# Two graph layers on one core: products read on the way from one growing bank, in a fixed order woven into the next stage

## The chip, the cores and the metric

The kernel runs on one core of a Trainium2 chip. TensorE (PE in the profile) multiplies, with its weight loads listed apart as PEld; VectorE (DVE), ScalarE (ACT) and GpSimd (POOL) do the element work; SyncE (SP) issues most of the transfers. The metric is the device time of one execution in microseconds (us). The kernel before took 1896.66 us, the median of three runs (1894.19 to 1897.85).

## The reference

For 64 graphs of 256 nodes with 512 features, an attention layer masked by the adjacency matrix and then a normalised graph convolution, each with a layer norm and a residual sum. Everything is float32.

```python
h = jnp.maximum(_layernorm(x, axis=-1), 0.0)
query = h @ Wq_w.T + Wq_b;  keyt = h @ Wk_w.T + Wk_b;  value = h @ Wv_w.T + Wv_b
weight = adj * jnp.exp(query @ keyt^T)
weight = weight / jnp.sum(weight, axis=2, keepdims=True)
x = x + weight @ value

h = jnp.maximum(_layernorm(x, axis=-1), 0.0)
A_hat = adj + I;  d = A_hat.sum(-1) ** -0.5
x = x + (A_hat * d[:, None] * d[None, :]) @ (h @ W + b)
```

(Shortened: batch indices left out.)

## The kernel before

**Pairs.** The 64 graphs go in 32 pairs (`NP`). The 512 rows of a pair lie in four tiles of 128 partitions. Query and key weights are merged once into one matrix, so that only one projection ("key", `m_set`) stands between the features and the scores; the value projection (`v_set`) and the graph weight (`w1_set`) are the other two.

**Seven products.** Each product of 512x512 matrices is done as seven products of half-size blocks instead of eight (the Winograd form of Strassen's method). Sums of blocks are made beforehand on both sides: S1 to S4 on the left, T1 to T4 on the right. The seven products are then added up in a fixed pattern. One product of a projection is 8 matmul records (4 matmuls in float32, two records each) of 128x256; one gather of the convolution, and one product of the scores, is 8 records of 128x128. The results lie in PSUM banks of 512 columns.

**How the sums were formed.** `seven_products` (L370) uses three banks. The first product P1 is copied out by ScalarE (`a1`). Later products land in other banks, and VectorE adds `a1` to two of them on the way (`s2`, `s3`, the temporaries U2 and U3), which are then added to the finished banks. For the keys (`key_side`, L385) the finished sums go into `gT` with a bias per row, for the values (`values`, L435) into `v`. In the convolution (`convolve`, L640) `gather` makes A_hat times h, transposed, in one bank that is read on the way (`chain`), and `product` multiplies by the graph weight; the results are scaled by the degree factor `d` and added to `x` by VectorE (L674) and GpSimd (L684).

**What runs beside it, per pair.**
- `measure`: layer-norm statistics of the next pair (`bn_stats`, `bn_aggr`), row sums of its adjacency (`degrees`), and the inverse roots on GpSimd (`inverse_root`, a chain of small operations); a small round trip through DRAM on SP for the degree row
- `normed`: relu of the layer norm on ScalarE, `h_a` for the first layer and `h_b` for the second
- `blocks_transposed` (`hq`) on VectorE and 16 `move_quadrants` copies on ScalarE: the transposed features `hT`
- `feature_sums`, `key_sums` and `neighbour_sums`: the block sums, on GpSimd from the second pair on (for the keys `eng = nc.vector if p == 0 else nc.gpsimd`)
- `key_terms` (`hc`, L281), `weighted_degrees` (`ad`, L597) and `add_graph_bias` (L614) on VectorE, each with two tensors in SBUF as its inputs
- `attend`: scores, exponentials on ScalarE, masks on VectorE, the output products (`pm_o`), and the residual sum; after it the diagonal of the adjacency is raised by one on GpSimd (L854)

**Order.** The program text is unrolled and a scheduler puts each engine's instructions in an order when the kernel is built; each engine then works its queue in that order. `tc.issue_after(ins)` keeps what is written inside it behind `ins` on that instruction's own engine, without a semaphore. Work for the neighbouring pairs is passed into the stages as callbacks (`then`, `then_u2`, ...), which write it down behind one of the stage's own reads. Nothing fixed the order of the matmuls of different stages against each other. In the loop, pair p attends, then pair p+1 is projected, then pair p is convolved.

**Buffers.** `x` has three, `a` (adjacency) and `hT` two, most temporaries one (`A0`, `A1`, `U2`, `U3`). The next adjacency load on SP waits for the last reader of its buffer, which is `weighted_degrees`; the next `x` load waits for the store of the pair that leaves.

Of the kernel before, what the change touches and what calls it, by code (L numbers as in the profile page):

```python
# [16 lines left out]
def kernel(  # L17
# [216 lines left out]
    last_root = [None]  # L234

    def inverse_root(src, plus, name):
# [4 lines left out]
        last_root[0] = nc.gpsimd.tensor_tensor(r, s, minus_half, ALU.pow).ins  # L241
        return r

    def scale_offset(p, name, scale=None):
# [3 lines left out]
        for t in range(TB):  # L248
            st = sm.tile([P, 6], F32, tag="st", name=f"st_{name}_{t}")
            nc.vector.bn_stats(st, xt[:, t, :])  # L250
            nc.vector.bn_aggr(mv[:, t, :], st)
# [24 lines left out]
    def key_terms(p, h):  # L276

        acc = sm.tile([P, TB], F32, tag="ka", name=f"ka_{p}")
        scratch = p1.tile([P, D], F32, tag="A0", name=f"hc_{p}")
# [48 lines left out]
    def key_sums(p, gT):  # L328
# [5 lines left out]
        eng = nc.vector if p == 0 else nc.gpsimd  # L334
# [5 lines left out]
        return (a11, a12, a22, s1, s2, a21, s4)  # L340

    def products_of(name, w, weight_moves):
# [6 lines left out]
        def product(bank, which, part, start):  # L349
# [3 lines left out]
            for r in range(2):  # L353
                for dt in range(2):
# [3 lines left out]
                    nc.tensor.matmul(  # L358
# [11 lines left out]
    def seven_products(name, w, parts, weight_moves, first, u2, c11, u3, c22, c21, c12):  # L370

        b11, b21, b22, t1, t2, t3, t4 = parts
        product = products_of(name, w, weight_moves)
        first(product(0, A11, b11, True))
        u2(product(1, S2, t2, True))
        c11(product(0, A12, b21, False))
        u3(product(1, S3, t3, False))
        c22(product(2, S1, t1, True))
        c21(product(1, A22, t4, False))
        return c12(product(2, S4, b22, False))  # L380

# [3 lines left out]
    def key_side(p, parts, then, then_u2, then_u3):  # L385
        gT = p1.tile([P, DC, NT], F32, tag="gT", name=f"gT_{p}")
        a1, s2, s3 = (temp(tag, f"g{p}") for tag in ("A1", "U2", "U3"))
# [4 lines left out]
        def block(i, g):  # L392
            return gT[:, 2 * i : 2 * i + 2, ts(g, N)]

        def first(pm):
            with tc.issue_after(nc.scalar.copy(a1, pm).ins):  # L396
                then()

        def u2(pm):
            with tc.issue_after(nc.vector.tensor_tensor(s2, pm, a1, add).ins):  # L400
                then_u2()

        def u3(pm):
            with tc.issue_after(nc.vector.tensor_tensor(s3, pm, a1, add).ins):  # L404
                then_u3()

        def c11(pm):
            for r in range(2):
                nc.scalar.activation(
                    block(0, 0)[:, r, :], pm[:, r, :], AF.Identity, bias=bias(0, r)  # L410
                )

        def into(i, g, pm, more):
# [375 lines left out]
    def nothing():  # L789
        pass  # L790
# [159 lines left out]
```

## Time and profile before

| | |
|---|---|
| median of three runs | 1896.66 us (1894.19 to 1897.85) |
| the profiled execution | 1896.71 us, span 1894.9 us |
| granted TensorE clock | 0.997 |
| VectorE busy | 1358.7 us, 72% |
| ScalarE busy | 797.9 us, 42% |
| GpSimd busy | 1070.3 us, 56% |
| PE, w products (L358) | 413.2 us, 1792 records of 386 ns |
| ACT, moves into hT (L311) | 305.5 us, 496 of 616 ns |
| DVE, hc (L281) | 115.9 us, 128 of 905 ns |
| DVE, graph bias (L614) | 94.5 us, 128 |
| POOL, idle before its first w sum (L708) | 410.1 us in 31 |

The span is the time from the first to the last instruction. The profile repeats itself: a pair takes 57.7 us from one key product to the next, from pair 2 to the last but one. The records of neighbouring matmuls overlap by some 0.16 us, since the end of each is modelled; for what a stage costs, the distance between starts is read. A figure in brackets behind a line is the idle time of that engine just before, and what ended it.

### The profile page before, as it was taken

To read this page: it belongs to the slowest core of one execution; us is meant where nothing else is said; L and a number is where in the kernel's file an instruction comes from. 1 tells how busy PE (TensorE), PEld (TensorE's weight loads), DVE (VectorE), ACT (ScalarE), POOL (GpSimd) and SP (SyncE) were. 2 spreads that over 40 slices of the span, in tenths; PEclk is the share of its full clock that TensorE was granted. 3 is DMA by queue.
4 is the path that set the end of the run, shared out by engine and by line. 5 is a ranking of instruction groups with operands and counts; after the bars stand their busy time and mean duration, and the time that the engine had idled before them with its cause. 6 is when DMAs were issued, how large, how long until landed. Compare 5 with 4: busy or idle time off the path is not lost.

```text
span 1894.9 us, 27986 instructions
## 1 busy us (share of the span) xinstructions
PE 1852.5 (98%) x10114; PEld 1642.0 (87%) x10114; DVE 1358.7 (72%) x3130; ACT 797.9 (42%) x1476; POOL 1070.3 (56%) x1191
## 2 busy tenths in 40 slices
PE   8999999999999999999999999999999999999997
PEld 7888888888888888888888888888888888888886
DVE  7877677677777676776777776777776767767764
ACT  3444443344444344434444443454344444434412
POOL 3545556646557555566465565555564555655544
PEclk9999999999999999999999999999999999999999
DMA  8243133332243432343422434413434323344011
GB/s 222 40 106 84 47 76 83 91 95 65 48 95 78 95 88 52 68 92 81 95 74 40 93 78 95 94 48 65 95 78 95 80 46 82 80 93 95 29 23 45
DMA packets 224266, 148.42 MB, mean 78 GB/s; under 512 B 150272, under 2 KB 170752, under 8 KB 224128
## 3 DMA queue, kind: packets, MB, share of 16 engines
q1 hardware_dynamic: 206112, 112.03, 22.3%
q0 software_dynamic: 16960, 33.56, 11.5%
q8 instruction: 80, 1.31, 0.3%
q10 hardware_dynamic: 1056, 1.05, 0.2%
q14 instruction: 58, 0.48, 0.1%
HBM read 112.99 MB, written 33.62 MB: 77 GB/s over the span
## 4 chain that ended last, share of the span: by engine, by line
PE 73%; DVE 25%; issue 1%; POOL 1%; DMA 1%; ACT 0%; DVEq 0%; ACTq 0%; POOLq 0%
PE pm_w L358 21%; PE pm_g L358 20%; PE pm_s L511 10%; PE pm_o L566 10%; DVE hc L281 6%; PE pm_v L358 6%; PE pm_l L654 5%; DVE hq L292 4%; DVE ad L597 3%; DVE x L614 2%; DVE wT L532 1%; DVE U_l L696 1%; DVE yS L694 1%; DVE U_v L446 1%; DVE v L472 1%; DVE v L471 1%
## 5 line engine op out<-in xcount | busy, mean ns | idle before, releaser
L358 PE MATMUL pm_w<-w_set,yS 128*128 128x256 f32 x1792 | 413.2, 386 | 3.8 <-DVE U_w L674 3.8
L358 PEld LDWEIGHTS pm_w<-w_set,yS 128*128 128x128 f32 x1792 | 332.4, 191 | 57.3 <-issue 10.4
L311 ACT COPY hT<-hq 32x512 f32<-32x512 f32 x496 | 305.5, 616 | 17.7 <-DVE hq L292 11.9
L708 POOL TENSOR_TENSOR yS<-yS 128x512 f32<-128x512 f32 x32 | 41.1, 1284 | 410.1 <-DVE yS L707 410.1
L358 PE MATMUL pm_v<-v_set,hT 128*128 128x256 f32 x1024 | 245.2, 382 | 10.3 <-DVE v L458 7.5
L358 PE MATMUL pm_g<-hT,m_set 128*128 128x256 f32 x1024 | 238.5, 381 | 4.2 <-DVE gT L415 4.2
L566 PE MATMUL pm_o<-v,wT 128*128 128x257 f32 (+1 forms) x1024 | 235.3, 382 | 3.5
L358 PEld LDWEIGHTS pm_v<-v_set,hT 128*128 128x128 f32 x1024 | 192.3, 190 | 47.5 <-DVE v L458 19.2
L566 PEld LDWEIGHTS pm_o<-v,wT 128*128 128x128 f32 x1024 | 189.1, 190 | 40.3 <-DVE wT L532 16.0
L358 PEld LDWEIGHTS pm_g<-hT,m_set 128*128 128x128 f32 x1024 | 195.7, 191 | 31.9 <-DVE gT L415 5.0
L358 PE MATMUL pm_g<-hS,m_set 128*128 128x256 f32 x768 | 181.2, 379 | 1.0 <-DVE U_g L404 1.0
L358 PE MATMUL pm_v<-v_set,hS 128*128 128x256 f32 x768 | 176.8, 379 | 0.0
L358 PEld LDWEIGHTS pm_g<-hS,m_set 128*128 128x128 f32 x768 | 145.7, 190 | 21.3 <-DVE U_g L404 1.4
L358 PEld LDWEIGHTS pm_v<-v_set,hS 128*128 128x128 f32 x768 | 146.0, 190 | 19.7
L674 DVE SCALAR_TENSOR_TENSOR x<-pm_w,irr_d,x 128x256 f32<-128x256 f32 x256 | 110.7, 475 | 52.1 <-PE pm_w L358 48.7
L684 POOL TENSOR_TENSOR x<-x,U_w 128x512 f32<-128x512 f32 x64 | 81.0, 1267 | 93.5 <-DVE U_w L674 93.5
L674 DVE SCALAR_TENSOR_TENSOR U_w<-pm_w,irr_d,A_w 128x256 f32<-128x256 f32 x128 | 56.0, 480 | 98.8 <-PE pm_w L358 98.8
L396 ACT COPY A_g<-pm_g 128x512 f32<-128x512 f32 x32 | 18.7, 585 | 245.2 <-PE pm_g L358 244.5
L281 DVE SCALAR_TENSOR_TENSOR hc<-h_a,c_all 128x512 f32<-128x512 f32 x128 | 115.9, 905 | 2.0
L267 ACT ACTIVATE h_b<-x,nb_b,rs_b 128x512 f32<-128x512 f32 x128 | 93.8, 803 | 47.9 <-POOL nb_b L260 47.9
L576 DVE SCALAR_TENSOR_TENSOR x<-pm_o,rsum,x 128x256 f32<-128x256 f32 x256 | 110.5, 474 | 1.1
L654 PE MATMUL pm_l<-aT,h_b 128*128 128x128 f32 x768 | 98.6, 278 | 10.6 <-DVE U_l L696 10.6
(157 smaller groups left out, 3342.8 us busy)
## 6 DMA issues: line engine op xcount, KB each, us to landing
x<-in_x_dram SPq DMA_DIRECT2D x64, 512.0 KB, 4.8
x<-in_L_gnn_Wv_b_dram POOLq DMA_DIRECT2D x32, 1024.0 KB, 10.5
out_dram<-x SPq DMA_DIRECT2D x62, 512.0 KB, 3.6
a<-in_adj_dram SPq DMA_DIRECT2D x64, 256.0 KB, 3.0
aq<-in_adj_dram SPq DMA_DIRECT2D x124, 128.0 KB, 5.4
drow<-dflat SPq DMA_DIRECT2D x32, 256.0 KB, 4.7
wq_rows<-in_L_gnn_Wq_w_dram ACTq DMA_DIRECT2D x2, 512.0 KB, 7.7
wk_rows<-in_L_gnn_Wk_w_dram SPq DMA_DIRECT2D x2, 512.0 KB, 7.0
```

Source lines behind the costliest of these rows:

```text
L267: nc.scalar.activation(h[:, t, :], x_tiles[p][:, t, :], AF.Relu, bias=nb[:, t : t + 1], scale=rd[:, t : t + 1],)
L281: nc.vector.scalar_tensor_tensor(scratch, h[:, t, :], 1.0, c_all, mult, mult, accum_out=acc[:, t : t + 1])
L292: nc.vector.transpose(hq[:, t, :], h[:, t, :])
L311: last = nc.scalar.copy(dst[j * Q : (j + 1) * Q, i], src[i * Q : (i + 1) * Q, j])
L358: nc.tensor.matmul(banks[bank][:, r, :], left[:, ts(r, P)], right, start=start and r == 0 and dt == 0, stop=r == 1 and dt == 1, skip_group ...
L511: nc.tensor.matmul(banks[bank][:, g, :], left[:, dt, ts(g, P)], right[:, dt, ts(g, P)], start=start and g == 0 and dt == 0, stop=g == 1 an ...
L566: nc.tensor.matmul(pm[:, 0:width], wT[:, kb, qb, g, :], v[:, kb * G + g, lo : lo + width], start=kb == 0, stop=kb == NB - 1,)
L576: nc.vector.scalar_tensor_tensor(xh, pm[:, 0:HD], rsum, xh, mult, add)
L597: nc.vector.scalar_tensor_tensor(scratch.rearrange("p (nb q) -> p nb q", q=P), a[:, t, :].rearrange("p (nb q) -> p nb q", q=P), 1.0, row_o ...
L654: nc.tensor.matmul(banks[bank][:, fi, g, :], left[:, g, ts(fi, P)], right[:, g, :], start=start and fi == 0 and g == 0, stop=fi == 1 and g ...
L674: last = nc.vector.scalar_tensor_tensor(dst[:, r, :], pm[:, r, :], dr_, plus[:, r, :], mult, add)
L684: last = nc.gpsimd.tensor_tensor(block(i, nb), block(i, nb), more, add).ins
```

## The change

The key and value projections no longer go through `seven_products`. A function `projections` writes both out in one fixed order. Per projection one bank grows: P1, then P1+P6, then P1+P6+P7 and so on are accumulated in it, and ScalarE copies the state out in between (`a`, `u2`, `u3`); the copies are added to the other banks by VectorE. The convolution's w products do the same with `wchain`. Every matmul of projections and convolution is kept behind the one before it in the text by `in_order`. The value projection's first product is placed among the keys, and the convolution of the pair before begins (two gathers) inside the value projection, by `filler`. Callbacks are replaced by a table of named places. The key sums are on VectorE for all pairs, `neighbour_sums` is split into `adjacency_sums` and `node_sums`, both on GpSimd, and graph bias, degree sums, statistics, the second norm, moves and weight sums have new places.

```diff
-        scratch = p1.tile([P, D], F32, tag="A0", name=f"hc_{p}")
+        scratch = p1.tile([P, D], F32, tag="U3", name=f"hc_{p}")
...
-        eng = nc.vector if p == 0 else nc.gpsimd
+        eng = nc.vector
+    last_product = [None]
+    def in_order(*args, **kwargs):
+        with tc.issue_after(last_product[0]) if last_product[0] else ExitStack():
+            last_product[0] = nc.tensor.matmul(*args, **kwargs).ins
...
-                    nc.tensor.matmul(
+                    in_order(
...
-    def seven_products(name, w, parts, weight_moves, first, u2, c11, u3, c22, c21, c12):
-        b11, b21, b22, t1, t2, t3, t4 = parts
-        product = products_of(name, w, weight_moves)
-        first(product(0, A11, b11, True))
-        u2(product(1, S2, t2, True))
-        c11(product(0, A12, b21, False))
-        u3(product(1, S3, t3, False))
-        c22(product(2, S1, t1, True))
-        c21(product(1, A22, t4, False))
-        return c12(product(2, S4, b22, False))
...
+        def key_sum(i, g, pm, more):
             for r in range(2):
                 last = nc.vector.scalar_tensor_tensor(
-                    block(i, g)[:, r, :], pm[:, r, :], bias(i, r), more[:, r, :], add, add
+                    key_block(i, g)[:, r, :], pm[:, r, :], bias(i, r), more[:, r, :], add, add
                 )
             return last
...
+        a, u2, u3 = (temp(tag, f"g{p}") for tag in ("A1", "U2", "U3"))
+        chain = keys_of(0, A11, b11, True)
+        behind(nc.scalar.copy(a, chain), "key P1")
+        rest = keys_of(2, S1, t1, True)
+        keys_of(0, S2, t2, False)
+        behind(nc.scalar.copy(u2, chain), "key P6")
+        side = keys_of(1, A12, b21, True)
+        behind(key_sum(0, 0, side, a), "key C11")
+        keys_of(0, S3, t3, False)
+        behind(nc.scalar.copy(u3, chain), "key P7")
+        behind(key_sum(1, 1, rest, u3), "key C22")
+        va = temp("A0", f"v{p}")
+        vchain = values_of(0, A11, b11, True)
+        nc.scalar.copy(va, vchain)
+        keys_of(0, A22, t4, False)
+        for r in range(2):
+            last = nc.scalar.activation(
+                key_block(1, 0)[:, r, :], chain[:, r, :], AF.Identity, bias=bias(1, r)
+            )
+        behind(last, "key C21")
+        keys_of(2, S4, b22, False)
+        last = key_sum(0, 1, rest, u2)
+        keys[p] = gT
+        behind(last, "key C12")
+        vu2, vu3 = (temp(tag, f"v{p}") for tag in ("A1", "U2"))
+        vrest = values_of(2, S1, t1, True)
+        values_of(0, S2, t2, False)
+        behind(nc.scalar.copy(vu2, vchain), "value P6")
+        vside = values_of(1, A12, b21, True)
+        behind(nc.vector.tensor_tensor(value_block(0, 0), vside, va, add), "value C11")
+        values_of(0, S3, t3, False)
+        behind(nc.scalar.copy(vu3, vchain), "value P7")
+        behind(nc.vector.tensor_tensor(value_block(1, 1), vrest, vu3, add), "value C22")
+        filler()
+        values_of(0, A22, t4, False)
+        nc.vector.tensor_copy(value_block(1, 0), vchain)
+        values_of(2, S4, b22, False)
+        nc.vector.tensor_tensor(value_block(0, 1), vrest, vu2, add)
...
-    def neighbour_sums(p, h, aT):
...
+    def adjacency_sums(p, aT):
...
+        nc.gpsimd.tensor_tensor(t1, b12, b11, sub)
+        nc.gpsimd.tensor_tensor(t2, b22, t1, sub)
+        nc.gpsimd.tensor_tensor(b12, b22, b12, sub)
+        nc.gpsimd.tensor_tensor(t4, b21, t2, sub)
+        return (b11, b21, b22, t1, t2, b12, t4)
+    def node_sums(p, h):
+        a11, a21 = h[:, 0:G, 0:HD], h[:, 0:G, HD:D]
+        a12, a22 = h[:, G:TB, 0:HD], h[:, G:TB, HD:D]
+        hbS = p1.tile([P, 3, G, HD], F32, tag="hbS", name=f"hbS_{p}")
+        s1, s2, s4 = (hbS[:, i] for i in range(3))
+        nc.gpsimd.tensor_tensor(s1, a21, a22, add)
+        nc.gpsimd.tensor_tensor(s2, s1, a11, sub)
+        nc.gpsimd.tensor_tensor(a21, a11, a21, sub)
+        last = nc.gpsimd.tensor_tensor(s4, a12, s2, sub)
+        if p == 0:
+            with tc.issue_after(last.ins):
+                weight_sums(w1_set, w1_21, nc.gpsimd)
+        return (a11, a12, a22, s1, s2, a21, s4)
+    def convolution(p, left_parts, right_parts, d, then):
...
+        def scaled(tag, pm, nb):
+            dst = temp(tag, f"w{p}")
+            for r in range(G):
+                last = nc.scalar.mul(dst[:, r, :], pm[:, r, :], factor(nb, r))
+            return dst, last
+        def into(i, nb, pm):
+            for r in range(G):
+                to = block(i, nb)[:, r, :]
+                last = nc.vector.scalar_tensor_tensor(
+                    to, pm[:, r, :], factor(nb, r), to, mult, add
+                )
             return last
...
-        chain = gather(0, a11, c11, True)
-        with tc.issue_after(moved) if moved else ExitStack():
-            nc.scalar.copy(b11, chain)
...
+        def more_into(i, nb, more):
+            return nc.gpsimd.tensor_tensor(block(i, nb), block(i, nb), more, add)
...
+        def begin():
+            chain = gather(0, a11, c11, True)
+            behind(nc.scalar.copy(b11, chain), "sum P1")
+            side = gather(1, a12, c21, True)
+            nc.vector.tensor_tensor(b11, side, b11, add)
+        def finish():
+            part, three = (temp(tag, f"l{p}") for tag in ("U3", "A0"))
+            chain = gather(0, s2, u2)
+            nc.vector.tensor_tensor(part, chain, b11, sub)
+            rest = gather(2, s1, u1, True)
+            gather(0, s3, u3)
+            nc.scalar.copy(three, chain)
+            wchain = product(0, A11, b11, True)
+            nc.vector.tensor_tensor(b22, rest, three, add)
+            nc.gpsimd.tensor_tensor(t2, b22, part, sub)
+            a, _ = scaled("A1", wchain, 0)
+            more_into(0, 0, a)
+            gather(0, a22, u4)
+            behind(nc.scalar.copy(b21, chain), "sum P4")
+            gather(2, s4, c22)
+            nc.vector.tensor_tensor(t2, t2, rest, sub)
+            nc.vector.tensor_tensor(t1, rest, part, add)
+            nc.gpsimd.tensor_tensor(t3, t2, b11, sub)
+            nc.gpsimd.tensor_tensor(t4, b21, t2, sub)
+            wside = product(1, A12, b21, True)
+            behind(into(0, 0, wside), "C11")
+            product(0, S2, t2, False)
+            s_, last = scaled("U2", wchain, 1)
+            behind(last, "P6")
+            more_into(0, 1, s_)
+            wrest = product(2, S1, t1, True)
+            behind(into(1, 1, wrest), "C22")
+            product(0, S3, t3, False)
+            u_, _ = scaled("U3", wchain, 1)
+            behind(more_into(1, 1, u_), "more")
+            product(2, S4, b22, False)
+            into(0, 1, wrest)
+            product(0, A22, t4, False)
+            into(1, 0, wchain)
+            if p == NP - 1:
+                for i, nb in ((0, 0), (1, 1), (0, 1), (1, 0)):
...
+    def measure_late(p):
+        with tc.issue_after(last_sums[f"b{p - 2}"]):
+            measure(p)
...
+    def move(p, first, last):
+        if first == 0:
+            hTs[p] = p2.tile([P, DC, NT], F32, tag="hT", name=f"hT_{p}")
+        move_quadrants(blocks[p], hTs[p], range(first, last))
...
+    def second_norm(p):
+        second[p] = node_sums(p, normed(p, f"b{p}", *norms[p]))
...
-    def project(p, then_g):
...
     def first_layer(p):
         attend(p, parts[p], key_parts[p], terms[p], aTs[p])
-        for t in range(TB):
+        for t in (2, 3, 0, 1):
             diag = aTs[p][:, t // G, t % G, ts(t // G, P)]
             last = nc.gpsimd.tensor_tensor(diag, diag, ident, add)
-        if p + 1 < NP:
-            with tc.issue_after(last.ins):
+        with tc.issue_after(last.ins):
+            if p + 1 < NP:
                 add_value_bias(p + 1)
+            sides[p] = adjacency_sums(p, aTs[p])
         norms[p] = scale_offset(p, f"b{p}", deg[p][0])
-    def second_layer(p, nxt):
-        def then_u3():
-            if nxt < NP:
-                aTs[nxt] = transposed_adjacency(nxt)
-        then_t2, then_first = nothing, nothing
+    def second_layer(p):
+        nxt = p + 2 if p < NP - 2 else NP
+        work = {
+            "sum P1": [(move, nxt, 4, 8)],
+            "sum P4": [(move, nxt, 8, 13)],
+            "C11": [(weigh_degrees, p + 1)],
+            "P6": [(move, nxt, 13, 16)],
+            "C22": [(turn_adjacency, nxt)],
+            "more": [(lambda q: parts.update({q: feature_sums(q, hTs[q])}), nxt)],
+        }
+        if p == NP - 2:
+            work["sum P4"] = [(second_norm, NP - 1)]
         if p == NP - 1:
-            then_t2 = lambda: add_graph_bias(p)
-        elif p == NP - 2:
-            then_first = lambda: finish_second_norm(NP - 1)
-        else:
-            then_first = ahead(move_second_half, nxt)
-        last = convolve(p, second[p], deg[p][0], moved.get(nxt), then_t2, then_first, then_u3)
-        if nxt < NP:
-            with tc.issue_after(last):
-                parts[nxt] = feature_sums(nxt, hTs[nxt])
-    def finish_second_norm(p):
-        second[p] = neighbour_sums(p, normed(p, f"b{p}", *norms[p]), aTs[p])
+            work["C11"] = [(add_graph_bias, p)]
+        return convolution(p, second[p], sides[p], deg[p][0], in_places(work))
+    def project(p):
+        finish = []
+        def filler():
+            if p < NP - 1:
+                begin, rest = second_layer(p - 1)
+                begin()
+                finish.append(rest)
+        work = {
+            "key P1": [(measure_late, p + 1)],
+            "key P6": [(second_norm, p - 1)],
+            "key C11": [(add_graph_bias, p - 1)],
+            "key C21": [(norm_features, p + 1)],
+            "key C12": [(turn_blocks, p + 1), (find_key_sums, p)],
+            "value P6": [(move, p + 1, 0, 4)],
+            "value C11": [(find_terms, p + 1)],
+        }
+        if p == 1:
+            work["key C22"] = [(turn_adjacency, 1)]
+        projections(p, parts[p], in_places(work), filler)
+        return finish
+    def project_first_pair(v21):
+        work = {
+            "key P1": [(lambda p: weight_sums(v_set, v21), 0), (find_terms, 0)],
+            "key P6": [(norm_features, 1)],
+            "key C22": [(turn_blocks, 1), (lambda p: deg.update({p: degrees(p)}), 1)],
+            "key C21": [(move, 1, 0, 6), (add_value_bias, 0)],
+            "key C12": [(find_key_sums, 0), (weigh_degrees, 0)],
+            "value P6": [(move, 1, 6, 10)],
+            "value P7": [(move, 1, 10, 16)],
+            "value C22": [(find_terms, 1)],
+        }
+        projections(0, parts[0], in_places(work), lambda: None)
...
     for p in range(NP):
         first_layer(p)
-        if p + 1 < NP:
-            project(p + 1, lambda: finish_second_norm(p))
         if p == NP - 1:
-            second_layer(p - 1, NP)
-        if p != NP - 2:
-            second_layer(p, p + 2)
+            for q in (p - 1, p):
+                for part in second_layer(q):
+                    part()
+        else:
+            for finish in project(p + 1):
+                finish()
```

## The prediction

> **What bounds it now.** I read the page first: TensorE (PE) is busy 98% of the span and nothing else passes 72%.
>
> ```profile
> PE 1852.5 (98%) x10114; PEld 1642.0 (87%) x10114; DVE 1358.7 (72%) x3130; ACT 797.9 (42%) x1476; POOL 1070.3 (56%) x1191
> ```
>
> So the most that can be won is what PE loses between matmuls. The chain of waits repeats every 57.7 us, one pair of graphs; I took the timeline of one such period, 880.81 to 938.52.
>
> ```profile
> 880.81 1.89 PE L358 MATMUL pm_g<-hT,m_set 128*128 128x256 f32 x8
> 882.54 1.89 PE L358 MATMUL pm_g<-hS,m_set 128*128 128x256 f32 x8
> ...
> 903.68 1.99 PE L358 MATMUL pm_v<-v_set,hT 128*128 128x256 f32 x8 [0.26 <-DVE v L458]
> ...
> 907.33 2.02 PE L654 MATMUL pm_l<-aS,hbS 128*128 128x128 f32 x16
> 909.67 1.13 PE L654 MATMUL pm_l<-aT,h_b 128*128 128x128 f32 x8 [0.31 <-DVE U_l L696]
> ...
> 931.20 7.49 PE L566 MATMUL pm_o<-v,wT 128*128 128x257 f32 x32
> 938.52 1.68 PE L358 MATMUL pm_g<-hT,m_set 128*128 128x256 f32 x7
> ```
>
> Starts count here, since ends overlap. A product (8 matmuls, 256 wide) takes 882.54-880.81 = 1.73 us, a gather (8 of 128) 0.89. Per period 200 wide matmuls at 0.216 and 112 narrow ones at 0.112 make 55.7 us; 57.7 is spent, **2.05 lost**: 0.53 at the last value product with the restart after it, 0.55+0.08 at the third gather (16 gather matmuls should take 1.79, not 2.34), 0.39 at the attention output (7.32 against 6.93 in the last pair, where no GpSimd (POOL) work runs beside the masks), 0.18 inside the w products, 0.4 in small pieces.
>
> Why the value product waits is the second thing to see:
>
> ```profile
> 901.38 1.63 DVE L281 SCALAR_TENSOR_TENSOR hc<-h_a,c_all 128x512 f32<-128x512 f32 x1
> 902.95 0.08 DVE L281 DVE_READ_ACCUMULATOR hc<-h_a,c_all 128x1 f32 x1
> 902.95 0.68 DVE L458 TENSOR_TENSOR v<-pm_v,U_v 128x512 f32<-128x512 f32 x1
> ```
> ```profile
> 900.74 1.73 POOL L339 TENSOR_TENSOR gS<-gT,gS 128x512 f32<-128x512 f32 x1
> ```
>
> An hc, 0.68 elsewhere, stands until POOL's key sum is over. VectorE (DVE) operations with both inputs in SBUF and POOL operations take turns; those that read PSUM or one SBUF input do not (statistics, 0.66-0.69 beside POOL sums at 888-889). The price shows in the graph bias, four operations in 2.73 us in the period, 5.77 at the end:
>
> ```profile
> 894.33 2.73 DVE L614 SCALAR_TENSOR_TENSOR x<-b_all,ds,x 128x512 f32<-128x512 f32 x4
> ```
> ```profile
> 1874.20 5.77 DVE L614 SCALAR_TENSOR_TENSOR x<-b_all,ds,x 128x512 f32<-128x512 f32 x4
> ```
> ```profile
> 1874.43 1.65 POOL L708 TENSOR_TENSOR yS<-yS 128x512 f32<-128x512 f32 x1 [8.25 <-DVE yS L707]
> 1876.04 1.71 POOL L709 TENSOR_TENSOR yS<-yS 128x512 f32<-128x512 f32 x1
> 1877.72 1.70 POOL L684 TENSOR_TENSOR x<-x,A_w 128x512 f32<-128x512 f32 x1
> ```
>
> In turns, each bias operation takes (5.77-0.68)/3 = 1.7 us instead of 0.66, starting with the one after POOL's arrival.
>
> **What the change gives PE.** Products into the growing bank need its copy out to be over. A copy starts 1.93 after its product starts (A_g, 882.74) and takes 0.58; another product always lies between, so the bank is free at 2.5 of 3.45 us: no wait, if ScalarE (ACT) is free then. Its new work per period (two copies more for keys, one for values, w scalings from PSUM at 0.46 as L409: about +1.9 us on 25) fits: the batches behind the copies (h_b 2.93, moves 0.62 each: 4, 4, 5, 3) end before the next copy is due, the tightest being u3, due at 8.83 and free at 8.9. POOL loses the four key sums (6.1 us) and gains one sum (1.28, as L708); it has 13 us idle ahead of L708 either way, worth nothing by itself. DVE gets the key sums at 0.61-0.69 each (the first pair runs them there, 48.28 to 50.9) and loses two key adds, one value add and four w scalings: about -1 us on 41.7. The copy of a 128x512 PSUM bank on DVE is not in the trace: 0.40 by L184 at half the width, 0.69 by the adds; I take 0.69, it has slack.
>
> So the value wait goes (-0.53): no POOL sum runs beside the hc's any more. The third gather (-0.45): `part` no longer queues behind the b11 add; it starts 1.15 after its gather, ends at 1.84, the bank is wanted at 1.79, 0.15 stays with the restart. The attention output (-0.39): POOL's diagonal adds now start with tiles 2 and 3, whose mask comes third, so none runs beside mask (1,0), and the feature sums end earlier; bounds 0 and -0.39. With 0.07 from the w product no longer split, **56.3** per period without new waits.
>
> **What it takes back.** Times from the first key product. PE wants `rest` for S4 at 7 products = 12.08; before it, key_sum(1,1) must have read it. That stands on DVE behind the four graph-bias operations, which now follow key_sum(0,0): queues run in the order of the program text when work is ready (in the first pair the key add gT, ready at 37.4, ran at 43.75, after transposes and a reduction traced ahead of it). key_sum(0,0) starts 7.1 (2.0 after its product, as L400), two halves 0.80, bias at 7.9, 8.6, 9.25, 9.9. Beside it h_b now starts behind the u2 copy at 5.9 and ends 8.9; then POOL's four node sums begin, the very operations the bias takes turns with. POOL is first in the roots: statistics end at 5.65 (1.8+3.86 as 885.15-889.01), 3.43 us as 893.02-896.45, so 9.2, later if the bias slows irr_d (1.54 beside it at 87.38). **The first node sum thus meets the bias at 9.0 to 9.5, the third bias starts at 9.25.** After it: one bias is blocked, ends 11.6, key_sum 12.4, PE waits 0.35. Before it: two are blocked, 12.6, 13.3, PE waits 1.3. I take 0.35, by the slowed irr_d; bounds 0 (ordered otherwise) and 1.3.
>
> The rule behind this is in the Trainium skill, page "SBUF — State Buffer", section "Who interferes with whom": whichever of the two starts first holds the shared ports for its whole instruction. The row agrees that the two take turns, but by the rule's full blocking a turn would cost 1.27+0.66 = 1.93 where the row has 1.7, and PE's wait would be 0.6 or 1.9.
>
> The other loss is in the w products; times from the second-part gathers. t4 on POOL ends 9.8. The four degree sums (ad, 0.42 alone, 1.37 beside a POOL sum at 77.39) now come after into(0,0), at 9.1: the first waits for t4, the third ends 11.1. The U2 scaling ends 10.87, more_into follows at 10.95 to 12.4 and blocks the fourth: 12.65, s and ds 13.1, into(1,1) 13.9. PE wants that bank for S4 at 13.26: 0.75 lost. Were the fourth ad first, nothing: bounds 0 and 0.75; I take 0.75, POOL being ready 0.3 before the fourth. Today the ad's run at 905-908 with POOL idle.
>
> Costed at nothing: statistics move 2.5 us forward; their x, issued at 931 (4.8 us to landing, done by 937.2), is wanted at 940.3; if late, DVE and then key_sum wait as long. Adjacency loads on SP follow the degree sums, some 10 us later; out and x loads queue behind them with 10 us to spare. Behind key C12 DVE has transposes 2.6, key sums 2.5, hc's 3.0, five adds 3.3 = 11.4 in the 13 us until `part`: no wait, but 0.5 if hc keeps today's mean 0.905.
>
> **Sum.** 56.3+0.35+0.75 = 57.4, -0.33 on the 29 equal periods between 130.67 and 1804.41 = -9.6. Start: PE loses some 8 us before 131 (the 2.98 at 81.76 from ad's beside node sums, 1.1 and 1.5 in the first pair beside the w1 sums); those move, but w1 sums then meet the pair-1 key sums: -4, bounds -8 and +1. End: 2.2, 1.2 and 3.84 are lost now, the last by the bias beside POOL; the unwoven last gathers lose 0.8 each, the bias still 1.2: -2, bounds -5 and +2. Span 1894.9-15.6 = 1879.3; the execution took 1.8 more (1896.71, as the median 1896.66): **1881 us**, own range 1868 to 1890 (one collision or the other at its bound).
>
> **Rivals.**
> 1. *Slower: node sums beat the third bias.* One mechanism: bias and node sums in turns ahead of key_sum(1,1), from POOL's start before 9.25. 56.3+1.3+0.75 = 58.35, +0.62 x 29 = +18, -6: 1909. For it: h_b ends 8.9 and the margin is 0.3; against: the roots hold POOL to 9.2 or more.
> 2. *No collision costs.* The engines' order falls otherwise or POOL comes later: -1.43 x 29 = -41, -6: 1849; with 0.35 left, 1859. For it: all else fits. Against: both overlaps follow from rows.
> 3. *DVE is the bound between key C12 and `part`*, 0.5 more per period on the forecast: the change then gives nothing, 1895. For it 11.4 of 13 us; against it, POOL idles there, so hc is 0.68.
>
> **Chances.** Forecast 0.36, rival 1 0.33, rival 2 0.21, rival 3 0.10. Runs spread 0.2%, about what a measurement can tell from no change. Faster: forecast and rival 2, 0.57; same: most of rival 3, 0.07; slower: rival 1 and the rest, 0.36. Range 1846 to 1912, rival 2 to rival 1.
>
> **What would show it.** The wait at the last value product gone; hc at 0.68. PE waiting at the last key product for gT: 0.35, 1.3 or none; L614's counterpart above 0.75 with node sums beside it. PE waiting at w's S4 for x, with an ad over 1 us ahead. Attention output near 6.93. The prediction is wrong if PE waits on ACT copies, or if a queue's order differs from the text's.

## The result, and the profile after

The changed kernel takes 1900.77 us (median of 12 runs, 1899.9 to 1902.06), the kernel before 1896.81 in the same comparison: ratio 1.0022, 95% interval [1.0013, 1.0031]. It is slower, by a little more than nothing. 1881 was forecast, so the sign was wrong. The profiled execution has a span of 1898.0 against 1894.9 before. (One execution of a later kernel, that with the diagonal order alone, took 4949.5 us where its three others took some 1887, and is left out of that kernel's median.)

The page's row of engines:

```profile
PE 1834.1 (97%) x10114; PEld 1636.7 (86%) x10114; DVE 1386.2 (73%) x3030; ACT 861.9 (45%) x1604; POOL 945.1 (50%) x1099
```

TensorE is busy for 18 us less than before in a span that is 3 us longer: less time goes into its stages and more into stops between them. The timeline of PE over one pair, 880.30 to 938.47, shows where (columns: start, duration, engine, line, operation, records, and in brackets the idle time before and what ended it):

```profile
880.30 1.89 PE L347 MATMUL pm_g<-hT,m_set 128*128 128x256 f32 x8
...
890.66 1.89 PE L347 MATMUL pm_g<-hS,m_set 128*128 128x256 f32 x8
893.87 1.99 PE L347 MATMUL pm_g<-hT,m_set 128*128 128x256 f32 x8 [1.32 <-DVE gT L401]
...
906.12 1.89 PE L347 MATMUL pm_v<-v_set,hT 128*128 128x256 f32 x8
907.85 1.95 PE L347 MATMUL pm_l<-aS,hbS 128*128 128x128 f32 x16
909.77 1.13 PE L347 MATMUL pm_l<-aT,h_b 128*128 128x128 f32 x8
...
914.25 7.12 PE L347 MATMUL pm_w<-w_set,yS 128*128 128x256 f32 x32
921.73 3.72 PE L347 MATMUL pm_w<-w_set,yS 128*128 128x256 f32 x16 [0.35 <-DVE x L667]
925.29 1.05 PE L489 MATMUL pm_s<-hT,gT 128*128 128x128 f32 x8
...
931.54 7.09 PE L544 MATMUL pm_o<-v,wT 128*128 128x257 f32 x32
938.47 1.89 PE L347 MATMUL pm_g<-hT,m_set 128*128 128x256 f32 x8
```

Read the distances between starts. The value products follow each other without a stop, the third gather starts 1.92 after the second pair of gathers (1.79 would be ideal, 2.34 before), and the attention output takes 938.47-931.54 = 6.93 (7.32 before). All three losses that the change was counted on to remove are gone, but for 0.13 at the third gather. Two new ones stand there: the last key product starts at 893.87, where 890.66+1.73 = 892.39 was possible, **1.48 late**, and its successor 0.10 more; the sixth w product, behind four that start at 914.25, starts at 921.73 instead of 914.25+4x1.73 = 921.16, **0.57 late**, and 0.10 more behind it. The figures in brackets are smaller than the lateness (1.32 and 0.35), since they count from the modelled end of the matmuls before, which lies 0.16 to 0.2 past the point where the next could have started.

What the key product waited for, VectorE's and GpSimd's timelines at the same place:

```profile
887.48 0.88 DVE L401 SCALAR_TENSOR_TENSOR gT<-pm_g,gb,A_g 128x256 f32<-128x256 f32 x2 [1.60 <-PE pm_g L347]
888.27 4.75 DVE L592 SCALAR_TENSOR_TENSOR x<-b_all,ds,x 128x512 f32<-128x512 f32 x4
892.95 0.86 DVE L401 SCALAR_TENSOR_TENSOR gT<-pm_g,gb,U_g 128x256 f32<-128x256 f32 x2
```
```profile
887.68 1.01 POOL L241 TENSOR_TENSOR irr_d<-irs_d,minus_half 128x4 f32<-128x4 f32 x1
888.66 0.42 POOL L260 TENSOR_TENSOR nb_a<-nm_a,irr_a 128x4 f32<-128x4 f32 x1
889.23 1.57 POOL L615 TENSOR_TENSOR hbS<-h_b 128x512 f32<-128x512 f32 x1 [0.16 <-ACT h_b L267]
890.88 1.60 POOL L616 TENSOR_TENSOR hbS<-hbS,h_b 128x512 f32<-128x512 f32 x1
892.44 1.71 POOL L618 TENSOR_TENSOR h_b<-h_b 128x512 f32<-128x512 f32 x1
```

Four graph biases (L592) take 4.75 us where 2.73 would do. Two run at their own pace, to about 889.7. The node sum of L615 came at 889.23, during the second of them, and holds the third back; the next sum holds back the fourth; and the key sum (the second L401), which frees the bank that PE wants, stands behind all four. The third bias by itself:

```profile
889.60 1.75 DVE L592 SCALAR_TENSOR_TENSOR x<-b_all,ds,x 128x512 f32<-128x512 f32 x1
```

The key sum is over at 892.95+0.86 = 893.81, and PE starts 0.06 later. This is rival 1 of the prediction, nearly to the number: a period of 58.17 where it said 58.35.

The times by stretch: 29 equal periods, each 0.45 longer in the mean, make +13.0 us; the start, up to the keys of pair 2, is 6.5 us shorter (124.14 against 130.67); the end 3.4 us shorter (87.1 against 90.5). 13.0-6.5-3.4 = 3.1, the difference of the spans.

### The profile page after: what moved, and what is told of

Read it like the earlier page. It is cut to its first block, busy times and chain, and to the rows that moved or that the text cites. A ratio compares the mean times of both kernels' runs of the same rounds, so it can differ in the third digit from the quotient of the medians.

```text
span 1898.0 us, 28019 instructions
## 1 busy us (share of the span) xinstructions
PE 1834.1 (97%) x10114; PEld 1636.7 (86%) x10114; DVE 1386.2 (73%) x3030; ACT 861.9 (45%) x1604; POOL 945.1 (50%) x1099
## 4 chain that ended last, share of the span: by engine, by line
PE 79%; DVE 19%; issue 1%; DMA 1%; DVEq 0%; ACTq 0%
PE pm_v L347 17%; PE pm_g L347 15%; PE pm_w L347 13%; PE pm_o L544 12%; PE pm_l L347 11%; PE pm_s L489 10%; DVE x L592 8%; DVE ad L575 5%; DVE gT L401 3%; DVE x L667 2%; PE pm_mT L176 1%; DMA wq_rows<-in_L_gnn_Wq_w_dram 1%; DVE s L584 0%; DVE hc L281 0%; DVE ds L586 0%
## 5 line engine op out<-in xcount | busy, mean ns | idle before, releaser
L347 PE MATMUL pm_w<-w_set,yS 128*128 128x256 f32 x1792 | 408.9, 383 | 14.7 <-DVE x L667 14.7
L694 POOL TENSOR_TENSOR yS<-yS,U_l 128x512 f32<-128x512 f32 x32 | 40.6, 1269 | 515.4 <-DVE yS L693 515.4
L347 PE MATMUL pm_v<-v_set,hT 128*128 128x256 f32 x1024 | 236.7, 379 | 0.0
L544 PE MATMUL pm_o<-v,wT 128*128 128x257 f32 (+1 forms) x1024 | 227.3, 379 | 0.0
L347 PE MATMUL pm_g<-hS,m_set 128*128 128x256 f32 x768 | 176.2, 379 | 0.0
L667 DVE SCALAR_TENSOR_TENSOR x<-pm_w,irr_d,x 128x256 f32<-128x256 f32 x256 | 111.9, 478 | 75.3 <-PE pm_w L347 75.3
L592 DVE SCALAR_TENSOR_TENSOR x<-b_all,ds,x 128x512 f32<-128x512 f32 x128 | 150.6, 1237 | 0.0
L798 POOL TENSOR_TENSOR aT<-aT,ident 128x128 f32<-128x128 f32 x128 | 66.0, 563 | 91.0 <-DVE wT L510 91.0
L575 DVE SCALAR_TENSOR_TENSOR ad<-a,drow 128x256 f32<-128x256 f32 x128 | 103.4, 808 | 3.4
L401 DVE SCALAR_TENSOR_TENSOR gT<-pm_g,gb,U_g 128x256 f32<-128x256 f32 x128 | 55.7, 475 | 65.1 <-PE pm_g L347 63.5
```

Of the source, the lines that this page charges most:

```text
L347: last_product[0] = nc.tensor.matmul(*args, **kwargs).ins
L401: last = nc.vector.scalar_tensor_tensor(key_block(i, g)[:, r, :], pm[:, r, :], bias(i, r), more[:, r, :], add, add)
L544: nc.tensor.matmul(pm[:, 0:width], wT[:, kb, qb, g, :], v[:, kb * G + g, lo : lo + width], start=kb == 0, stop=kb == NB - 1,)
L575: nc.vector.scalar_tensor_tensor(scratch.rearrange("p (nb q) -> p nb q", q=P), a[:, t, :].rearrange("p (nb q) -> p nb q", q=P), 1.0, row_o ...
L592: nc.vector.scalar_tensor_tensor(xt[:, t, :], b1_all, ds[p][:, t : t + 1], xt[:, t, :], mult, add)
L667: last = nc.vector.scalar_tensor_tensor(to, pm[:, r, :], factor(nb, r), to, mult, add)
```

## The experiments

All ratios are to the kernel before, run on the same chip in the same comparison.

### The node sums left out

```diff
-        hbS = p1.tile([P, 3, G, HD], F32, tag="hbS", name=f"hbS_{p}")
-        s1, s2, s4 = (hbS[:, i] for i in range(3))
-        nc.gpsimd.tensor_tensor(s1, a21, a22, add)
-        nc.gpsimd.tensor_tensor(s2, s1, a11, sub)
-        nc.gpsimd.tensor_tensor(a21, a11, a21, sub)
-        last = nc.gpsimd.tensor_tensor(s4, a12, s2, sub)
+        s1, s2, s4 = a21, a11, a12
         if p == 0:
-            with tc.issue_after(last.ins):
-                weight_sums(w1_set, w1_21, nc.gpsimd)
+            weight_sums(w1_set, w1_21, nc.gpsimd)
```

> The four block sums of h on GpSimd are left out (blocks of h stand in for them); the graph bias stays where the change put it. Theory of turns (the bias waits for node sums): the bias operations fall from 1.24 to about 0.75 us, TensorE's wait before the last key product (1.48 of start delay, 0.10 restart) is gone in every pair, the period goes from 58.2 to 56.6, the span from 1898 to about 1849. Rival, queue length (four bias operations ahead of the key sum are too many even alone): bias at 0.75 or not, the wait stays over 1 us and the span above 1885.

Measured: 1848.32 us, ratio 0.974 [0.9724, 0.9757]. The key product's wait is gone, the biases take 0.750 in the mean instead of 1.237, and the wait at the w products is 0.35 in a period, as before. So all of the key wait comes from the meeting of bias and node sums, and without it the change is worth 2.6%.

### The bias split, so that the two don't meet

```diff
-    def add_graph_bias(p):
+    def add_graph_bias(p, tiles=range(4)):
...
-            nc.vector.tensor_tensor(part, chain, b11, sub)
+            behind(nc.vector.tensor_tensor(part, chain, b11, sub), "part")
...
+        if p < NP - 1:
+            work["part"] = [(add_graph_bias, p, (2, 3))]
...
-            "key C11": [(add_graph_bias, p - 1)],
+            "key C11": [(add_graph_bias, p - 1, (0, 1))],
```

> Two of the four bias operations stay behind the first key sum, two move behind part in the convolution, where GpSimd is idle. Theory of turns: all four take about 0.75 us, the key wait is gone, period 56.6, span about 1849; the 0.57 at the w products stays. Rival, VectorE's queue up to the third gather is full, so the work only moves: part or b22 come late, a new wait of 0.5 to 1.3 at the gathers, span 1865 to 1890.

Measured: 1851.22 us, ratio 0.9755 [0.974, 0.9769]. Nothing is left out here, so this is a kernel that beats both. PE's waits for VectorE, in the whole span (columns: total us, times, longest), first in the changed kernel and then in this one:

```profile
PE pm_g L347 <- DVE gT L401: 40.8, 31, 1.3
PE pm_w L347 <- DVE x L667: 14.7, 31, 4.1
```
```profile
PE pm_w L347 <- DVE x L667: 14.8, 31, 4.1
```

The line of the keys has vanished, that of the w products hasn't moved. The period is 56.59, 1.58 less, which is the 1.48 and the 0.10 of the timeline.

### The node sums later: does the order of arrival decide?

The prediction's choice was between one bias held back and two, by which came first, the third bias or the first node sum. One or two idle roots ahead of the node sums, of the form and size of `irr_d`, should shift that arrival and nothing else (`range(2)` in the second kernel).

```diff
+        if p < NP - 1:
+            idle = sm.tile([P, TB], F32, tag="rs", name=f"idle_{p}")
+            for _ in range(1):
+                nc.gpsimd.tensor_tensor(idle, norms[p][0], minus_half, ALU.pow)
         nc.gpsimd.tensor_tensor(s1, a21, a22, add)
```

> The changed kernel with one root more (128x4, 1.01 us as irr_d) on GpSimd ahead of the node sums, its result unused: the first node sum comes at 9.9 instead of 8.9, behind the third bias (9.4), which is the case that the prediction took. If which of the two comes first decides, as the prediction's working has it: one turn instead of two, the last key product waits 0.35 instead of 1.48 with its restart 0.1, so 29 x 1.1 = 33 us less than the changed kernel: 1867. If the node sums block the bias however late they come, or if they are themselves on the path: 1901 or more.

> Two such roots: the first node sum comes at 10.9, behind the fourth bias (9.4 + 0.7). No turn is left and the last key product waits for nothing: 1849 to 1853, as where the node sums were left out or the bias was split, although GpSimd does more work and the node sums end 2 us later. If the later node sums are wanted earlier than that: above 1867.

Measured: 1900.5 (ratio 1.0017 [1.0007, 1.0026]) with one, 1871.5 (0.9862 [0.9848, 0.9877]) with two. Both missed what was expected, for one reason that the timelines show. GpSimd with one root:

```profile
884.78 1.01 POOL L618 TENSOR_TENSOR idle<-rs_b,minus_half 128x4 f32<-128x4 f32 x1
886.48 0.23 POOL L239 TENSOR_SCALAR irs_a<-mv_a 128x4 f32<-128x4 f32 x1 [0.69 <-DVE mv_a L251]
...
889.74 1.58 POOL L619 TENSOR_TENSOR hbS<-h_b 128x512 f32<-128x512 f32 x1 [0.15 <-ACT h_b L267]
```

The added root had its input early, so it was put ahead of the other roots, into a gap in which GpSimd waits for statistics; 0.69 of the gap was still left. The arrival did not move: 889.74 is 8.9 after the first key product (880.8), as without the root, and the wait of the last key product is the same 1.32 as there. Two roots fill the gap and push the rest by half a microsecond. VectorE, GpSimd and PE there:

```profile
874.96 3.75 DVE L592 SCALAR_TENSOR_TENSOR x<-b_all,ds,x 128x512 f32<-128x512 f32 x4
```
```profile
874.85 1.01 POOL L241 TENSOR_TENSOR irr_d<-irs_d,minus_half 128x4 f32<-128x4 f32 x1
...
876.38 1.78 POOL L619 TENSOR_TENSOR hbS<-h_b 128x512 f32<-128x512 f32 x1
```
```profile
877.35 1.89 PE L347 MATMUL pm_g<-hS,m_set 128*128 128x256 f32 x8
879.55 1.99 PE L347 MATMUL pm_g<-hT,m_set 128*128 128x256 f32 x8 [0.31 <-DVE gT L401]
```

The third bias by itself:

```profile
876.28 0.75 DVE L592 SCALAR_TENSOR_TENSOR x<-b_all,ds,x 128x512 f32<-128x512 f32 x1
```

Now the third bias starts at 876.28 and the node sum comes at 876.38, 0.10 behind. It is the node sum that is held (1.78 instead of 1.27), one bias only is held back after it, and the key product is 879.55-877.35-1.73 = 0.47 late. So the second kernel is by accident the very case that the prediction took for the change. Its period is 57.16, between 58.17 and 56.59. 0.45 us in GpSimd's arrival is worth 1.0 us a pair, 29 us in all; GpSimd's extra work itself did not show as a cost (1900.5 with one root, 1900.8 without).

### The degree sums elsewhere

Ahead of the add that PE waits for at the w products (L667, at 920.80), VectorE has the degree sums, and the last of them stands beside a GpSimd sum, 1.43 where the two before it take 0.42; VectorE and GpSimd in the changed kernel:

```profile
919.06 1.43 DVE L575 SCALAR_TENSOR_TENSOR ad<-a,drow 128x256 f32<-128x256 f32 x1
```
```profile
918.93 1.27 POOL L673 TENSOR_TENSOR x<-x,U_w 128x512 f32<-128x512 f32 x1 [1.14 <-ACT U_w L661]
```

The first try moved the four sums as they are, behind the add that PE waits for; alone, and with the split bias:

```diff
-            "C11": [(weigh_degrees, p + 1)],
...
-            "C22": [(turn_adjacency, nxt)],
+            "C22": [(weigh_degrees, p + 1), (turn_adjacency, nxt)],
```

> Only the four degree sums (ad) move from behind the first w sum to behind the second (into(1,1)). Theory of turns: TensorE's 0.57 us at w's sixth product is gone, period 57.6, span about 1880; the key wait of 1.48 is unchanged. Rival, the w products wait for the scaling on ScalarE or for the GpSimd adds themselves: the wait stays, span 1895 to 1900.

> Both moves together. Theory of turns: the two waits were independent, so the gains add: period about 56.0, span about 1830, 0.966 of the kernel before. Rival, a next wait stands close behind each (scaled copies on ScalarE, t3 and t4 on GpSimd): period 56.6 or more, span 1850 or more.

Measured: 1921.7 alone (1.0131 [1.0112, 1.0151]), 1867.33 with the split bias (0.9837 [0.9823, 0.9852]), each 16 to 21 us worse than without the move. The waits at the w products are gone in both traces; what came instead is seen on VectorE, in the kernel with this move alone:

```profile
940.92 1.37 DVE L575 SCALAR_TENSOR_TENSOR ad<-a,drow 128x256 f32<-128x256 f32 x1
...
942.62 0.82 DVE L584 TENSOR_TENSOR s<-s,irr_d 128x4 f32<-128x4 f32 x1
...
960.75 0.69 DVE L250 BATCH_NORM_STATS2 st_a<-x 128x6 f32<-128x512 f32 x1 [2.37 <-DMA x<-in_x_dram]
```

Two things went wrong. The sums meet other GpSimd work there: the fourth takes 1.37, and the addition of 128x4 behind it 0.82 instead of 0.16, so that a score product waits for VectorE 0.35 in 30 of the pairs. This takes back what the w products gained: a pair whose `x` is in time takes 58.16 here, as in the changed kernel. And in every second pair the statistics wait for their `x`. SP's queue shows where this starts, first the changed kernel, then this one:

```profile
920.52 0.89 SPq L93 DMA_DIRECT2D a<-in_adj_dram  x2
...
926.04 0.90 SPq L728 DMA_DIRECT2D out_dram<-x  x2
...
930.57 1.27 SPq L88 DMA_DIRECT2D x<-in_x_dram  x2
```
```profile
945.25 0.89 SPq L728 DMA_DIRECT2D out_dram<-x  x2
946.19 2.14 SPq L93 DMA_DIRECT2D a<-in_adj_dram  x2
...
951.44 0.91 SPq L88 DMA_DIRECT2D x<-in_x_dram  x2
```

The adjacency loads wait for the degree sums. Where these end early, the loads go out 5.5 us ahead of the store; where they end late, they go out between the store and the load of `x`, which is issued 0.06 after the store has landed. The `x` load was issued 9.6 us ahead of its first reader (940.20) in the changed kernel, 6.9 ahead (958.38, when the reader was ready) here, and took a median of 10.1 us to land in this stretch instead of 4.3. The place of the adjacency loads alone does not make it that slow: in the pair before, in the same order, the `x` load landed in a median of 5.5. What differs is a third transfer, the 1 MB of value biases that GpSimd adds into another `x` (L777). In this stretch, then in the pair before with its `x` load, then in the changed kernel:

```profile
950.03 1.33 POOL L777 DMA_DIRECT2D x<-in_L_gnn_Wv_b_dram  x1
```
```profile
891.86 1.36 POOL L777 DMA_DIRECT2D x<-in_L_gnn_Wv_b_dram  x1
```
```profile
891.95 0.89 SPq L88 DMA_DIRECT2D x<-in_x_dram  x2
```
```profile
931.93 1.33 POOL L777 DMA_DIRECT2D x<-in_L_gnn_Wv_b_dram  x1
```

It goes out 1.4 us ahead of the `x` load where that takes 10.1 us, and 0.1 ahead or 1.4 behind where it takes 5.5 or 4.3. From the first store on, in both traces with this move, the first of a pair's two `x` loads takes 7.6 us or more wherever GpSimd's load is 1.0 us or more ahead, and 5.7 or less everywhere else. So the late degree sums make the adjacency loads late, these the store (5.7 instead of 4.0 us for its second half), and the `x` load then comes behind GpSimd's. This is read from the traces; no run moved GpSimd's load alone. The prediction had named SP's queue and counted 10 us to spare; moving the degree sums spent them.

The second try splits the sums like the bias, and puts two of them where GpSimd stands idle (with `U2` as their scratch buffer in place of `A0`) and the last two where they were, so that the loads stay early:

```diff
-            "C11": [(weigh_degrees, p + 1)],
+            "C11": [(weigh_degrees, p + 1, (2, 3))],
...
-            work["part"] = [(add_graph_bias, p, (2, 3))]
+            work["part"] = [(add_graph_bias, p, (2, 3)), (weigh_degrees, p + 1, (0, 1))]
```

> The split bias, and the degree sums split in the same way: tiles 0 and 1 behind `part`, where GpSimd stands idle, tiles 2 and 3 where they were. The first two then take 0.4 each, and only the last meets a GpSimd sum, so into(1,1) is not late and the wait of 0.36 with its restart goes: 1851 - 30 x 0.4 = 1839. If the 1 us more on VectorE behind `part` delays the adds of the convolution and with them a product: 1851 or more, with a wait at the w products for yS.

Measured: **1828.04 us** (1827.8 to 1828.79), ratio 0.9633 [0.9617, 0.9649], the best of all. The first degree sum of each half on VectorE, of which only the second meets a GpSimd sum, and PE's w products:

```profile
879.47 0.42 DVE L580 SCALAR_TENSOR_TENSOR ad_U<-a,drow 128x256 f32<-128x256 f32 x1
...
885.71 0.97 DVE L580 SCALAR_TENSOR_TENSOR ad_A<-a,drow 128x256 f32<-128x256 f32 x1
```
```profile
882.85 10.57 PE L347 MATMUL pm_w<-w_set,yS 128*128 128x256 f32 x48
```

The six w products run through as one group. The period is 55.96; 200 wide and 112 narrow matmuls alone make 55.7. It gained 23 us on the split bias instead of the 12 expected: the expectation took the 0.36 in brackets, but the period shrank by 0.63, lateness and restart together, 19 us in 30 pairs, and one wait of 4.1 at the end went too.

### Single parts of the change

**Key sums back on GpSimd** in the changed kernel:

```diff
-        eng = nc.vector
+        eng = nc.vector if p == 0 else nc.gpsimd
```

> The changed kernel with the four key sums back on GpSimd (all pairs but the first, as before the change). If they made the value product wait, hc and sums in turns: 0.53 a period comes back, 1917, with a wait of a value product for VectorE. If the fixed order alone took that wait away, since another product now lies between: 1901.

Measured: 1903.5 us, ratio 1.0035 [1.0022, 1.0048], 2.7 us above the changed kernel and not 16. The period is 58.17 as there; the profiled execution has one longer one, of 61.04. The value products still follow each other without a stop:

```profile
905.22 1.89 PE L347 MATMUL pm_v<-v_set,hS 128*128 128x256 f32 x8
906.95 1.89 PE L347 MATMUL pm_v<-v_set,hT 128*128 128x256 f32 x8
```

In this kernel GpSimd's last key sum ends at 902.8, and only one hc is stretched by it (0.86; the mean is 0.747, 0.905 before the change). So in the changed kernel the value wait stays away wherever the key sums run. **And the reverse, key sums on VectorE in the kernel before**, with the same line changed the other way:

> The kernel before with the four key sums on VectorE for every pair, and nothing else. If GpSimd's sums standing in hc's way made the last value product wait, 0.53 a period goes: 1897 - 30 x 0.53 = 1881. Without a fixed order of the products the program puts the first gathers ahead of the last value products, since the key sums come sooner, so that VectorE's work behind the gathers and the values may collide: 1897 or more, with new waits of PE for VectorE at the value products or the gathers. Then the sums alone gain nothing and it is the order that takes the value wait away.

Measured: 1913.06 us, ratio 1.0094 [1.0077, 1.0111]. The products came in another order, gathers ahead of the last value products, the value wait is gone, and PE waits at the gathers for ScalarE instead:

```profile
915.63 0.39 PE L654 MATMUL pm_l<-aS,hbS 128*128 128x128 f32 x2
917.02 1.80 PE L654 MATMUL pm_l<-aS,hbS 128*128 128x128 f32 x14 [1.01 <-ACT yS L692]
```

The move alone loses 17 us in the old kernel and leaves the period of the new one as it is: what it is worth depends on the order of products that it is built into.

**The diagonal order alone**, in the kernel before:

```diff
-        for t in range(TB):
+        for t in (2, 3, 0, 1):
...
-        if p + 1 < NP:
-            with tc.issue_after(last.ins):
+        with tc.issue_after(last.ins):
+            if p + 1 < NP:
```

> The kernel before with GpSimd's diagonal adds in the order 2, 3, 0, 1 and the rest behind all four, as in the change, and nothing else. If the adds beside the masks made the attention output take 7.32 us: it takes 6.93, a pair's period is 0.39 shorter, 31 x 0.39 = 12 us: 1885. If the output is held by the masks alone: 1897.

> The same kernel as the one with the diagonal order alone, for its profile: if the order is what shortens the attention output, its 32 matmuls take 6.93 from start to the next start where the kernel before takes 7.32. It gained 8 us of the 12 that this would give; if the output takes 6.93 in all pairs, some 0.13 a period is given back elsewhere, at the value or the third gather; if it takes about 7.06, the masks keep the rest.

Measured: 1887.9 us (three executions of 1885.7 to 1887.93), ratio 0.9953 [0.9937, 0.997]. The profile is of a further execution, 1884.49 beside 1894.76:

```profile
924.71 7.10 PE L566 MATMUL pm_o<-v,wT 128*128 128x257 f32 x32
931.64 1.89 PE L358 MATMUL pm_g<-hT,m_set 128*128 128x256 f32 x8
```

931.64-924.71 = 6.93, in a period of 57.32 instead of 57.70: the whole 0.38, given back nowhere in the pair. The 8 us of the medians is less than the 12 of 31 periods, and the further execution's 10 lies between; the spans of the two traces, 1894.9 and 1882.7, differ by 12. Executions of the kernel before lie between 1894.1 and 1900.1, so single ones can't settle a difference of this size.

## Why the prediction was wrong

**The step that failed** is "The first node sum thus meets the bias at 9.0 to 9.5, the third bias starts at 9.25 ... I take 0.35, by the slowed irr_d". In the trace the node sum comes at 889.23-880.30 = 8.93, and the third bias at 889.60-880.30 = 9.30. What was wrong is the time of the roots, 3.43 and more. Both rows behind it, from the kernel before, have `irr_d` slowed by biases:

```profile
894.74 1.20 POOL L241 TENSOR_TENSOR irr_d<-irs_d,minus_half 128x4 f32<-128x4 f32 x1
```
```profile
87.38 1.54 POOL L241 TENSOR_TENSOR irr_d<-irs_d,minus_half 128x4 f32<-128x4 f32 x1
```

In the first, within the 3.43, `irr_d` began 0.41 behind the first of the biases (894.33), in the second 0.10 behind (87.28). In the change it begins 0.59 ahead of the first bias (887.68 and 888.27) and takes 1.01, and the roots take 3.11 in all. They are through at 8.8, and `h_b`, at 8.9 as foreseen, was then the later one by 0.16. A duration was carried over from a row without asking which of the two had started first there, in a place where just that was in question. The range of this step named both outcomes, and the two lay on different sides of no change; the margin of 0.3 us could not carry a forecast of the sign. The kernel with two idle roots is the forecast's case, and it ran in 1871.5.

**The terms**, per period, forecast and measured:

| term | forecast | measured | shown by |
|---|---|---|---|
| base without new waits | 56.3 | 55.96 | both split |
| key product behind the bias | 0.35 (bound 1.3) | 1.58 | changed kernel against the split bias |
| the same, node sum second | 0.35 | 0.57 | two idle roots against the split bias |
| w product behind the ad | 0.75 | 0.63 | both split against the split bias |
| period | 57.4 | 58.17 | changed kernel |

Of the 1.58, 0.06 is PE's start after the release and 0.10 the slower product after the wait. The differences, -0.34+1.23-0.12, make up the +0.77 of the period, 22 us in 29 of them. Start and end were taken too small, -4 and -2 against -6.5 and -3.4, which gives 4 us back: 1881+22-4 = 1899.

**What was right.** Both collisions, their places and their victims; value wait, third gather (0.13 left of it, 0.15 foreseen) and attention output; ScalarE's copies, which PE never waits for; VectorE's order as the text has it. **Right with a wrong reason**: the value wait went, but "no POOL sum runs beside the hc's any more" isn't why, since it stayed away with the key sums on GpSimd in the changed kernel. The order of products and copies, with other matmuls between a bank's uses, is what remains of the change there; that it is the cause was not tried by itself. **Sizes**: the waits for new collisions were worked out up to the release, without the 0.06 until PE starts and the 0.10 that the product after a wait takes longer. Some sums do not come out as written: 5.65+3.43 is 9.08 and not 9.2, which would have put the roots' end ahead of 9.25 by more; 12.6+0.80 is 13.4 and not 13.3; the w product's loss is 13.9-13.26 = 0.64 by its own times, not 0.75, and 0.63 was measured; two turns by the rule make 1.8, not 1.9; the losses listed for the period add up to 2.13, not 2.05. And the own range of 1868 to 1890 does not hold what is given as its reason: the key product's bound of 1.3 alone adds 0.95x29 = 28 us to 1881.

**The rivals.** Rival 1 is what happened, by its mechanism: the two experiments that part bias from node sums take 49 to 52 us off. Rival 2's 1849 was the price without the key collision (1848 and 1851), though it was meant to be without either; without either it is 1828. Rival 3 did not show: hc has a mean of 0.683, and PE does not wait there.

**On the shared turn.** The Trainium skill, page "SBUF — State Buffer", section "Who interferes with whom", says that the engine that issues first has the pair of ports for its whole instruction, and that issue order decides who is blocked. The idle roots agree on the order: 0.45 us of arrival changed which engine stood still. On the price the rows differ from the sum by full blocking, 1.27+0.66 = 1.93 a turn: node sums beside the biases follow each other at 1.65 and 1.56 (889.23, 890.88, 892.44). The lateness that turns made, 1.48 and 0.47, or 1.42 and 0.41 without the 0.06 of PE's start, lies between what the prediction had by rows (1.3 and 0.35) and by the rule (1.9 and 0.6), nearer the rows.

## What to carry to other kernels

When two outcomes of one race have prices of opposite sign, find which operation starts first by its own chain in the new schedule; a duration from a row with the race run the other way settles nothing. The cheap remedy is not to shift the race but to part its runners: half of a batch moved to where the other engine is idle took 50 us and then 23 off a kernel that looked finished. Before moving work that releases a buffer, follow the loads behind it in the queue: moved late, the degree sums cost 16 to 21 us by the loads behind them, more than the wait that they had made.

## What the runs showed of the hardware

- A GpSimd root of 128x4 that begins 0.11 ahead of a VectorE bias (874.85 and 874.96) takes its 1.01 and leaves the bias at its pace; begun 0.10 behind one, it took 1.54. A VectorE operation of 128x4 (`s`, 0.16 alone) stood 0.82 beside a GpSimd sum (942.62, inside 941.97 to 943.42).
- The two 512 KB loads of `x` took a median of 10.1 us to land where GpSimd's load of 1 MB had been issued 1.4 us ahead of them, 4.3 where it came 1.4 behind. Adjacency loads just ahead, with GpSimd's load at the same time, left them at 5.5.
